# Time mixing of each 128 rows moved into a later attention loop, in a Perceiver block in float32

## The chip, the cores and the metric

The kernel runs on one core of a Trainium2 chip. The metric is the device time of one execution in microseconds (us); lower is better. Before the change the median of three runs is 2709.6 us (2709.19 to 2710.01).

The engines that matter are TensorE (PE, with its weight loads, PEld), VectorE (DVE), ScalarE (ACT), GpSimd (POOL) and SyncE (SP), which issues nearly all DMAs. Each engine works through its own queue in order. Work that passes between engines waits on semaphores, which the Tile framework places.

## The reference

One Perceiver block: cross-attention, RWKV time mixing, and a feed-forward network (FFN), each behind a layer norm without gain and each added back to x. x is (32, 64, 256), the context is (32, 1601, 192), everything is float32.

```python
x = x + xattn(layernorm(x), ctx)          # 16 heads of 64, 1601 keys of 192
x = x + rwkv(layernorm(x))
x = x + ffn(layernorm(x))                 # relu(x @ w1 + b1) @ w2 + b2, width 1024

# xattn: q = query @ w_q, kv = ctx @ w_kv, softmax(q k^T / 8) v, then @ w_out + b_out
# rwkv:  shifted = x one step later in time (zeros first)
k_in = x * mix_k + shifted * (1 - mix_k)  # v_in and r_in likewise
k, v = k_in @ Wk.T, v_in @ Wv.T
r = sigmoid(r_in @ Wr.T)
td = exp(-exp(time_decay))
for t in range(64):
    e, ek = exp(time_first + k[t]), exp(k[t])
    wkv[t] = (num + e * v[t]) / (den + e)
    num, den = td * num + ek * v[t], td * den + ek
out = (r * wkv) @ Wo.T + bo
```

## The kernel before

x lies in SBUF for the whole run as `x_sb`, 16 tiles of 128 rows. One tile holds two batches of 64 queries.

**Queries** (to about 143.8 us). Four groups of 512 rows are normed, transposed and projected, and each head's query is multiplied with that head's key weights (`wkT`), so that the scores can be made from the 192 columns of the context itself. The folded queries go to DRAM (`q_dram`). `rstd_of` (L97) makes the inverse root of a variance: DVE adds epsilon, ACT takes the root, DVE the reciprocal. The constants of the time mixing (`rw_T`, `td_rows`, `omm`, `cols`) are made here too.

**Attention** (143.8 to 2485.44 us). The loop runs over 64 units u. Unit u is half a batch: b = u // 2, and of its 16 heads eight, j = u % 2, so 512 columns. Four units make a tile of x. The body of the loop works on two units at once, in this order of program:

- `last.total()`: DVE sums the exponentials of the unit before (L419, L421).
- `scores(u)`: six groups of 256 keys. Each has eight matmuls into a PSUM tile of two banks (L350; two such tiles, `ps_s`), a copy to SBUF by ACT (L357) and a running maximum by DVE (L359, L361). A seventh, small group holds the last 65 keys (L369). After the second group (i == 1) a hook is called, which runs `vproj` of the unit before the last, if that unit ended a tile.
- Loads of the next batch's context blocks and queries by SP.
- `max_all`: GpSimd takes the maximum over partitions (L387).
- `last.av_lo`: 13 chunks of keys, exponentials of the unit before times the first 128 context columns, into one PSUM bank `o_lo` (L432).
- `exps`: DVE subtracts the maximum (L393), ACT takes exponentials (L396, L399).
- `ctx_prep` for every second unit: DVE transposes the next batch's context (L257, L258).
- `last.av_hi`: the last 64 context columns into `o_hi` (L444, L454).
- `last.out`: the copies of `o_lo` (ACT, L473) and `o_hi` (DVE, L471) to `oT`, the denominators `den` by two matmuls (L477), and their reciprocal `rden` (L484).
- `vproj`, for every fourth unit u and two units later in the loop: 32 matmuls with the value weights into `v_ps` (L497), division by the denominators (L505), eight with the output weights into `y_ps` (L508), and two adds that bring the result into `x_sb` (L515, L516).

`den`, `v_ps` and `y_ps` share one PSUM pool, `ps_m`, of two banks, through the helper `bank`. With `ps_s` (four banks) and `o_lo` and `o_hi` all eight banks are in use.

**The tail** (2485.44 us to the end). Four stages of 512 rows (four tiles): `rwkv(nb)` does the time mixing of a stage, `ffn(nb)` the feed-forward, and the mixing runs one stage ahead. Within `rwkv` the order is norm (L584), transposes (L590) into `xp`, three mixed inputs (ACT `tmp` L609, DVE `in_` L612), projections (L621), exponentials (L642, L643), a sigmoid (L649), scans by DVE (L654), a reciprocal (L661), the products (L662, L663), and the output projection `ry` (L668), added into `x_sb`. `ffn` norms and transposes, makes `h_ps` (L689), the relu (L696), `fy` (L701), and writes the sums out by SP.

Program order on each engine is the order in which the instructions are written out; the framework moves nothing.

Of the kernel before, what the change touches and what calls it, by code (L numbers as in the profile page):

```python
# [9 lines left out]
F32 = mybir.dt.float32  # L10
# [5 lines left out]
P = 128  # L16
# [4 lines left out]
def kernel(  # L21
# [33 lines left out]

    nc = tc.nc
# [27 lines left out]
    nc.gpsimd.memset(ones, 1.0)  # L84

# [11 lines left out]
    def rstd_of(dst, var):  # L97
        nc.vector.tensor_scalar(dst, var, EPS, None, ALU.add)
        nc.scalar.activation(dst, dst, AF.Sqrt)
        nc.vector.reciprocal(dst, dst)  # L100
# [12 lines left out]
    with tc.tile_pool(name="aw", bufs=1) as aw:  # L113
        wv_lo = aw.tile([P, INNER], F32, name="wv_lo")
        wv_hi = aw.tile([P, INNER], F32, name="wv_hi")
        wo_sb = aw.tile([P, INNER // P, D], F32, name="wo_sb")

        with ExitStack() as st_a:
            cpool = st_a.enter_context(tc.tile_pool(name="ctx", bufs=1))

            kp = st_a.enter_context(tc.tile_pool(name="keys", bufs=2))
# [210 lines left out]
            ap = st_a.enter_context(tc.tile_pool(name="attn", bufs=1))  # L332
            ps_s = st_a.enter_context(tc.tile_pool(name="ps_s", bufs=2, space=PSUM))
            ps_o = st_a.enter_context(tc.tile_pool(name="ps_o", bufs=1, space=PSUM))
            ps_m = st_a.enter_context(tc.tile_pool(name="ps_m", bufs=2, space=PSUM))
# [4 lines left out]
            def scores(u, cT, q, hook):  # L340
# [4 lines left out]
                for i in range(KC // 2):  # L345
# [16 lines left out]
                    if i == 1:  # L362
                        hook()
# [159 lines left out]
            oT = rden = None  # L523
            for u in range(2 * B):
                b, j = divmod(u, 2)

                def finish(done=late):
                    if done is not None:
                        done.vproj()
# [3 lines left out]
                s_sb, mx = scores(u, cT, q_tiles[b], finish)  # L533
# [7 lines left out]
                if j == 0 and b + 1 < B:  # L541
                    cT_next = ctx_prep(b + 1)
                elif j == 1:
                    cT = cT_next
                if last is not None:
                    last.av_hi()
                    last.out()
                if j == 0:
                    c_tiles[b] = ctx_load(b)
# [5 lines left out]
            late.vproj()  # L555
            last.total()
            last.av_lo(0, NCK)
            last.av_hi()
# [3 lines left out]
    NB = 4  # L562
    TB = NT * P // NB
    BB = TB // T
    TT = TB // P
    NF = FF // P
    wp = ctx.enter_context(tc.tile_pool(name="fw", bufs=1))
    rp = ctx.enter_context(tc.tile_pool(name="rw", bufs=1))
    fp = ctx.enter_context(tc.tile_pool(name="ff", bufs=2))
    pp_t = ctx.enter_context(tc.tile_pool(name="pp_t", bufs=2, space=PSUM))  # L570
    pp_m = ctx.enter_context(tc.tile_pool(name="pp_m", bufs=4, space=PSUM))
    pp_y = ctx.enter_context(tc.tile_pool(name="pp_y", bufs=2, space=PSUM))

    w1_sb = wp.tile([P, 2, FF], F32, name="w1_sb")
    w2_sb = wp.tile([P, NF, D], F32, name="w2_sb")
    nc.sync.dma_start(w1_sb, w1.rearrange("(c p) f -> p c f", p=P))
    nc.sync.dma_start(w2_sb, w2.rearrange("(c p) d -> p c d", p=P))

    def normed(nb, name, dst):
        tiles = [nb * TT + k for k in range(TT)]  # L580
        mv, rstd = stats_of(fp, tiles, f"{name}_{nb}")
        xn = fp.tile([P, TT, D], F32, tag="xn", name=f"xn_{name}_{nb}")
        for k, i in enumerate(tiles):
            nc.vector.tensor_scalar(  # L584
                xn[:, k, :], x_sb[:, i, :], mv[:, k, 0:1], rstd[:, k : k + 1], ALU.subtract, ALU.mult
            )
        for c in range(2):
            pt = pp_t.tile([P, TT, P], F32, tag="t", name=f"xT_{name}_{nb}_{c}")
            for k in range(TT):
                nc.tensor.transpose(pt[:, k, :], xn[:, k, c * P : (c + 1) * P], ident)  # L590
            dst(c, pt)

    def rwkv(nb):
        xp = rp.tile([P, 2, BB, T + 1], F32, tag="xp", name=f"xp_{nb}", bufs=2)
        nc.gpsimd.memset(xp[:, :, :, 0:1], 0.0)

        def put(c, pt):
            nc.scalar.copy(
                xp[:, c, :, 1 : T + 1], pt.rearrange("p k (b t) -> p (k b) t", t=T)
            )  # L600

        normed(nb, "ln2", put)

        mixed = []
        for n, nm in enumerate(("k", "v", "r")):
            tmp = rp.tile([P, 2, BB, T], F32, tag="tmp", name=f"tmp_{nm}_{nb}", bufs=2)
            mi = rp.tile([P, 2, BB, T], F32, tag=f"in_{nm}", name=f"in_{nm}_{nb}", bufs=2)
            for c in range(2):
                nc.scalar.activation(  # L609
                    tmp[:, c], xp[:, c, :, 0:T], AF.Copy, scale=omm[:, n, c : c + 1]  # L610
                )
                nc.vector.scalar_tensor_tensor(  # L612
                    mi[:, c], xp[:, c, :, 1 : T + 1], cols[:, 2 + n, c : c + 1], tmp[:, c],
                    ALU.mult, ALU.add,
                )
            mixed.append(mi.rearrange("p c b t -> p c (b t)"))

        def proj(src, w, c, nm):
            ps = pp_m.tile([P, TB], F32, tag="mm", name=f"{nm}_ps_{nb}_{c}")
            for hc in range(2):  # L620
                nc.tensor.matmul(  # L621
                    ps,
                    lhsT=rw_T[w][:, hc, c * P : (c + 1) * P],
                    rhs=src[:, hc, :],
                    start=(hc == 0),
                    stop=(hc == 1),
                )
            return ps

        rw = rp.tile([P, 2, TB], F32, tag="rwv", name=f"rwv_{nb}", bufs=2)  # L630
        num = rp.tile([P, 2, BB, T + 1], F32, tag="num", name=f"num_{nb}")
        den = rp.tile([P, 2, BB, T + 1], F32, tag="den", name=f"den_{nb}")
        nc.gpsimd.memset(num[:, :, :, 0:1], 0.0)
        nc.gpsimd.memset(den[:, :, :, 0:1], 0.0)
        ek = rp.tile([P, 2, TB], F32, tag="ek", name=f"ek_{nb}")
        e = rp.tile([P, 2, TB], F32, tag="e", name=f"e_{nb}")
        ekv = rp.tile([P, 2, TB], F32, tag="ekv", name=f"ekv_{nb}")
        ev = rp.tile([P, 2, TB], F32, tag="ev", name=f"ev_{nb}")
        r = rp.tile([P, 2, TB], F32, tag="r", name=f"r_{nb}")
        for c in range(2):  # L640
            pk = proj(mixed[0], "Wk", c, "k")
            nc.scalar.activation(ek[:, c], pk, AF.Exp)  # L642
            nc.scalar.activation(e[:, c], pk, AF.Exp, bias=cols[:, 1, c : c + 1])  # L643
            pv = proj(mixed[1], "Wv", c, "v")
            nc.vector.tensor_tensor(ekv[:, c], ek[:, c], pv, ALU.mult)
            nc.vector.tensor_tensor(ev[:, c], e[:, c], pv, ALU.mult)
        for c in range(2):
            pr = proj(mixed[2], "Wr", c, "r")
            nc.scalar.activation(r[:, c], pr, AF.Sigmoid)  # L649
        for c in range(2):  # L650
            for b in range(BB):
                ts = slice(b * T, (b + 1) * T)
                for acc, src in ((num, ekv), (den, ek)):
                    nc.vector.tensor_tensor_scan(  # L654
                        acc[:, c, b, 1 : T + 1], td_rows[:, c, :], src[:, c, ts], 0.0, ALU.mult, ALU.add
                    )
            ev3 = ev[:, c].rearrange("p (b t) -> p b t", t=T)
            e3 = e[:, c].rearrange("p (b t) -> p b t", t=T)
            nc.vector.tensor_tensor(ev3, ev3, num[:, c, :, 0:T], ALU.add)
            nc.vector.tensor_tensor(e3, e3, den[:, c, :, 0:T], ALU.add)  # L660
        nc.vector.reciprocal(e, e)  # L661
        nc.vector.tensor_tensor(ev, ev, e, ALU.mult)  # L662
        nc.vector.tensor_tensor(rw, r, ev, ALU.mult)  # L663
        for k in range(TT):
            i = nb * TT + k
            py = pp_y.tile([P, D], F32, tag="y", name=f"ry_{nb}_{k}")
            for c in range(2):
                nc.tensor.matmul(  # L668
                    py,
                    lhsT=rw[:, c, k * P : (k + 1) * P],  # L670
                    rhs=rw_T["Wo"][:, c, :],
                    start=(c == 0),
                    stop=(c == 1),
                )
            nc.vector.tensor_tensor(x_sb[:, i, :], x_sb[:, i, :], py, ALU.add)
            nc.vector.tensor_tensor(x_sb[:, i, :], x_sb[:, i, :], bias_rows[:, 1, :], ALU.add)
# [37 lines left out]
    for nb in range(NB):  # L714
        if nb + 1 < NB:
            rwkv(nb + 1)
# [50 lines left out]
```

## Time and profile before

| | before |
|---|---|
| median of 3 runs | 2709.6 us (2709.19 to 2710.01) |
| the profiled execution: its own time | 2708.48 us |
| its span, first to last instruction | 2706.6 us |
| mean granted TensorE clock | 0.992 |
| busy in the span: PE / DVE / ACT / POOL | 2634.8 / 1891.5 / 974.8 / 122.9 us |
| queries, 0 to 143.80: PE busy | 123.12 us |
| attention, 143.80 to 2485.44: PE busy | 2329.17 of 2341.64 us, clock 1.00 |
| tail, 2485.44 to 2706.60: PE busy | 182.55 of 221.16 us, clock 0.93 |

The profile is of one execution, so its rows add up to its own time and not to the median. A group of instructions is shown with its line, engine, operation, output and inputs, number, total busy time and mean length of one, and the idle time that came just ahead of its instructions on their engine, with what ended it ("<-"). In a view by stretch, each engine has its busy time and, in brackets, its number of instructions; PEclk is the share of full clock that TensorE was granted. PE counts matmuls and transposes; the weight loads beside them are PEld.

### The profile page before, as it was taken

The page shows a single profiled execution, that of the slowest core. Times are in us where ns is not written, and L with a number is a line of the kernel's source. Part 1 is how long each engine was busy: PE and PEld are TensorE (multiplying, and loading weights), DVE is VectorE, ACT ScalarE, POOL GpSimd, SP SyncE. Part 2 cuts the span into 40 slices and gives each one's busy share as a digit, 9 for nine tenths or more (in the row PEclk, how much of TensorE's full clock was granted, in tenths as well). Part 3 has the DMA queues.
Part 4 walks back from the last instruction along what each step waited for, and adds up shares of the span by engine and source line. Part 5 has one row for each costly group of instructions (what it writes and reads, how often), then busy time and mean ns, then how long its engine had stood idle before and what let it go on. Part 6 is the DMA issues. An engine that isn't in the chain of part 4 may idle for free.

```text
span 2706.6 us, 27923 instructions
## 1 busy us (share of the span) xinstructions
PE 2634.8 (97%) x11424; PEld 1209.8 (45%) x11424; DVE 1891.5 (70%) x1983; ACT 974.8 (36%) x958; POOL 122.9 (5%) x92
## 2 busy tenths in 40 slices
PE   7979999999999999999999999999999999999699
PEld 3334444444444444444444444444444444444366
DVE  4467677776767776767677776767776767776864
ACT  2233333333333333323333333333333333333242
POOL 1000000000000000000000000000000000000000
PEclk9989999999999999999999999999999999999899
DMA  8983233332333331333333333333332323100000
GB/s 207 267 154 59 39 61 61 61 58 46 61 61 61 61 61 43 61 57 55 48 61 61 50 55 60 61 61 61 57 58 49 61 48 55 38 19 31 0 16 16
DMA packets 435279, 169.27 MB, mean 63 GB/s; under 512 B 330192, under 2 KB 421360, under 8 KB 435152
## 3 DMA queue, kind: packets, MB, share of 16 engines
q1 hardware_dynamic: 434272, 166.05, 32.4%
q8 instruction: 89, 1.46, 0.2%
q10 hardware_dynamic: 544, 1.05, 0.1%
q0 software_dynamic: 336, 0.40, 0.1%
q14 instruction: 38, 0.31, 0.0%
HBM read 138.60 MB, written 27.26 MB: 61 GB/s over the span
## 4 chain that ended last, share of the span: by engine, by line
PE 93%; DVE 4%; ACT 1%; issue 1%; DMA 1%; SPq 0%; POOL 0%; DVEq 0%; POOLq 0%; ACTq 0%
PE s_ps L350 37%; PE o_lo L432 27%; PE o_hi L444 13%; PE s_ps_r L369 3%; PE y_ps L508 2%; PE v_ps L497 2%; PE fy L701 2%; PE q_ps L192 2%; PE h_ps L689 1%; PE o_hi L454 1%; PE den L477 1%; DVE e L661 1%; PE ql_ps L208 1%; DMA q_dram<-q_hi 1%; PE qh_ps L223 0%
## 5 line engine op out<-in xcount | busy, mean ns | idle before, releaser
L350 PE MATMUL s_ps<-q,cT 64*128 64x512 f32 x4608 | 1013.5, 594 | 12.9 <-ACT s_sb L357 12.1
L357 ACT COPY s_sb<-s_ps 128x1024 f32<-128x1024 f32 x384 | 388.5, 1012 | 981.2 <-PE s_ps L350 981.2
L432 PE MATMUL o_lo<-s_sb,c 128*128 128x512 f32 (+1 forms) x1664 | 731.4, 596 | 0.0
L350 PEld LDWEIGHTS s_ps<-q,cT 64*128 64x128 f32 x4608 | 440.5, 187 | 549.8 <-issue 535.8
L361 DVE TENSOR_TENSOR m<-m,s_sb 128x1024 f32<-128x1024 f32 x256 | 313.7, 1225 | 368.3 <-ACT s_sb L357 368.3
L396 ACT ACTIVATE s_sb<-s_sb 128x2048 f32<-128x2048 f32 x192 | 366.7, 1911 | 454.3 <-DVE s_sb L393 454.3
L393 DVE TENSOR_TENSOR s_sb<-s_sb,mb 128x2048 f32<-128x2048 f32 x192 | 428.5, 2287 | 101.3 <-POOL mb L387 101.3
L432 PEld LDWEIGHTS o_lo<-s_sb,c 128*128 128x128 f32 (+1 forms) x1664 | 311.0, 190 | 392.0 <-issue 392.0
L444 PE MATMUL o_hi<-s_sb,c 128*64 128x512 f32 x1536 | 343.7, 596 | 0.0
L421 DVE TENSOR_TENSOR t<-t,s_sb 128x1024 f32<-128x1024 f32 x256 | 312.2, 1219 | 14.7 <-DVE t L421 0.5
L387 POOL PARTITION_ALL_REDUCE mb<-mx x64 | 114.2, 1785 | 2313.3 <-DVE mx L380 2313.3
L444 PEld LDWEIGHTS o_hi<-s_sb,c 128*64 128x64 f32 x1536 | 104.6, 137 | 231.2 <-issue 207.0
L359 DVE TENSOR_TENSOR m<-s_sb 128x1024 f32<-128x1024 f32 x64 | 78.4, 1225 | 92.7 <-ACT s_sb L357 92.6
L484 DVE RECIPROCAL rden<-den 128x256 f32<-128x256 f32 x64 | 111.8, 1748 | 0.0
L369 PE MATMUL s_ps_r<-q,cT 64*65 64x256 f32 x768 | 93.6, 376 | 0.0
L257 DVE STREAM_TRANSPOSE cT<-cb 128x768 f32<-128x768 f32 x96 | 92.7, 968 | 0.0
L419 DVE TENSOR_TENSOR t<-s_sb 128x1024 f32<-128x1024 f32 x64 | 77.7, 1214 | 0.0
L369 PEld LDWEIGHTS s_ps_r<-q,cT 64*65 64x65 f32 x768 | 54.0, 134 | 52.8 <-issue 33.5
L192 PE MATMUL q_ps<-xnT,wq_sb 128*128 128x512 f32 x128 | 60.5, 615 | 0.0
L508 PE MATMUL y_ps<-wo_sb,outT 128*128 128x256 f32 x256 | 59.5, 386 | 0.0
L689 PE MATMUL h_ps<-xT,w_sb 128*128 128x512 f32 x128 | 56.1, 594 | 0.6 <-ACT xT L682 0.6
L701 PE MATMUL fy<-w_sb,hT 128*128 128x256 f32 x256 | 55.9, 379 | 0.0
(124 smaller groups left out, 1415.2 us busy)
## 6 DMA issues: line engine op xcount, KB each, us to landing
q<-q_dram SPq DMA_DIRECT2D x64, 768.0 KB, 6.7
c<-in_ctx_dram SPq DMA_DIRECT2D x32, 1152.0 KB, 6.3
cb<-in_ctx_dram SPq DMA_DIRECT2D x192, 104.0 KB, 4.3
cb<-in_ctx_dram SPq DMA_DIRECT2D x192, 96.0 KB, 3.3
q_dram<-q_lo SPq DMA_DIRECT2D x16, 1024.0 KB, 8.8
q_dram<-q_hi SPq DMA_DIRECT2D x32, 256.0 KB, 6.8
x_sb<-in_x_dram SPq DMA_DIRECT2D x4, 512.0 KB, 8.6
w_sb<-in_L_ffn_w_dram SPq DMA_DIRECT2D x2, 1024.0 KB, 4.9
```

Of the source, the lines that this page charges most:

```text
L192: nc.tensor.matmul(pq, lhsT=wq_sb[:, c, hp * P : (hp + 1) * P], rhs=xnT[:, c, :], start=(c == 0), stop=(c == 1),)
L350: nc.tensor.matmul(ps[:, k, :], lhsT=cT[rs, s, i * P : (i + 1) * P], rhs=q[rs, s, js : js + HALF], start=(s == 0), stop=(s == NS - 1),)
L357: nc.scalar.copy(s_sb[:, 2 * i : 2 * i + 2, :], ps)
L361: nc.vector.tensor_tensor(m2, m2, s_sb[:, 2 * i : 2 * i + 2, :], ALU.max)
L369: nc.tensor.matmul(ps[0:KR, k, 0:HH], lhsT=cT[rs, s, NB1 * BL : KT + 1], rhs=q[rs, s, js + k * HH : js + (k + 1) * HH], start=(s == 0), st ...
L387: nc.gpsimd.partition_all_reduce(mb, mx, P, bass_isa.ReduceOp.max)
L393: nc.vector.tensor_tensor(s4, s4, mb.unsqueeze(1).to_broadcast([P, 4, HALF]), ALU.subtract)
L396: nc.scalar.activation(s4, s4, AF.Exp)
L421: nc.vector.tensor_tensor(t2, t2, p[:, 2 * i : 2 * i + 2, :], ALU.add)
L432: nc.tensor.matmul(self.po, lhsT=self.ctx[0:n, self.at[c], 0:P], rhs=self.s_sb[0:n, c, :], start=(c == 0), stop=(c == NCK - 1),)
L444: nc.tensor.matmul(self.ph[o * C2 : (o + 1) * C2, :], lhsT=self.ctx[:, self.at[c], P:C], rhs=self.s_sb[:, c, :], start=(c < 2), stop=False ...
L508: nc.tensor.matmul(py, lhsT=outT[:, k, :], rhs=wo_sb[:, k, :], start=(k == 0), stop=(k == NP - 1),)
```

## The change

- **`rstd_of`**: after DVE's add, GpSimd raises the variance to the power -0.5 with a constant tile `root`. ACT's root and DVE's reciprocal are gone. This holds for all layer norms.
- **Time mixing by tile.** `rwkv` is replaced by a class `Mixing` for one tile of 128 rows (two batches). It has five steps: `norm`, `mix`, `project`, `scan`, `out`. For tiles 0 to 14 they are put into the attention loop. Tile i's attention is complete when `vproj` has run in unit 4i+5; `norm` is at the end of that unit, `mix` in unit 4i+6 after the third group of scores (i == 2 in `scores`), `project` in unit 4i+7 between `av_lo` and `av_hi`, `scan` in the same unit after `out`, and `out` in unit 4i+8 after the third group of scores. `out` of tile 14 is behind the loop, between the last `av_lo` and `av_hi`.
- **PSUM of the mixing.** `mix`, `project` and `out` take their PSUM tiles from `ps_m`, the two banks that `den`, `v_ps` and `y_ps` also use. The projections of a tile are one bank for Wk, one for Wv and one for Wr.
- **Sigmoid.** r * wkv with r = 1 / (1 + exp(-k_r)) becomes a longer denominator: (1 + exp(-r)) * (e + den), with one reciprocal.
- **FFN.** The tail holds four `ffn` stages. Tile 15's mixing and the norms of stages 1 to 3 are called between pairs of its h matmuls, through the list `between`. Its PSUM is one bank for transposes, three for `h_ps`, two for `fy`.
- **Pools.** The SBUF pool of the mixing (`rw`) is opened ahead of attention; the attention weights (`aw`) move into the attention's own pools and are freed with them; `ps_m` stays open to the end.

The core of the diff (the removed `rwkv`, and the parts of the FFN that only moved, are cut):

```diff
+    root = const.tile([P, 4], F32, name="root")
+    nc.gpsimd.memset(root, -0.5)
...
     def rstd_of(dst, var):
         nc.vector.tensor_scalar(dst, var, EPS, None, ALU.add)
-        nc.scalar.activation(dst, dst, AF.Sqrt)
-        nc.vector.reciprocal(dst, dst)
+        nc.gpsimd.tensor_tensor(dst, dst, root[:, 0 : dst.shape[1]], ALU.pow)
...
+            class Mixing:
+                def __init__(self, i):
+                    self.i = i
+
+                def norm(self):
+                    i = self.i
+                    mv, rstd = stats_of(rp, [i], f"ln2_{i}")
+                    self.xn = rp.tile([P, D], F32, tag="xn", name=f"xn_ln2_{i}")
+                    nc.vector.tensor_scalar(
+                        self.xn, x_sb[:, i, :], mv[:, 0, 0:1], rstd[:, 0:1], ALU.subtract, ALU.mult
+                    )
+
+                def mix(self):
+                    i = self.i
+                    pt = bank([P, 2, 2, T], f"xT_ln2_{i}")
+                    for c in range(2):
+                        nc.tensor.transpose(pt[:, c, :, :], self.xn[:, c * P : (c + 1) * P], ident)
+                    xp = rp.tile([P, 2, 2, T + 1], F32, tag="xp", name=f"xp_{i}")
+                    nc.gpsimd.memset(xp[:, :, :, 0:1], 0.0)
+                    nc.scalar.copy(xp[:, :, :, 1 : T + 1], pt)
+                    self.mixed = []
+                    for n, nm in enumerate(("k", "v", "r")):
+                        tmp = rp.tile([P, 2, 2, T], F32, tag="e", name=f"tmp_{nm}_{i}")
+                        mi = rp.tile([P, 2, 2, T], F32, tag=f"in_{nm}", name=f"in_{nm}_{i}")
+                        for c in range(2):
+                            nc.scalar.activation(
+                                tmp[:, c], xp[:, c, :, 0:T], AF.Copy, scale=omm[:, n, c : c + 1]
+                            )
+                            nc.vector.scalar_tensor_tensor(
+                                mi[:, c], xp[:, c, :, 1 : T + 1], cols[:, 2 + n, c : c + 1],
+                                tmp[:, c], ALU.mult, ALU.add,
+                            )
+                        self.mixed.append(mi.rearrange("p c b t -> p c (b t)"))
+
+                def project(self):
+                    i = self.i
+
+                    def proj(n, w):
+                        ps = bank([P, 2, 2, T], f"{w}_ps_{i}")
+                        for c in range(2):
+                            for hc in range(2):
+                                nc.tensor.matmul(
+                                    ps[:, c, :, :],
+                                    lhsT=rw_T[w][:, hc, c * P : (c + 1) * P],
+                                    rhs=self.mixed[n][:, hc, :],
+                                    start=(hc == 0),
+                                    stop=(hc == 1),
+                                )
+                        return ps
+
+                    shape = [P, 2, 2, T]
+                    pk = proj(0, "Wk")
+                    pv = proj(1, "Wv")
+                    self.ek = rp.tile(shape, F32, tag="in_k", name=f"ek_{i}")
+                    self.e = rp.tile(shape, F32, tag="e", name=f"e_{i}")
+                    nc.scalar.activation(self.ek, pk, AF.Exp)
+                    for c in range(2):
+                        nc.scalar.activation(
+                            self.e[:, c], pk[:, c], AF.Exp, bias=cols[:, 1, c : c + 1]
+                        )
+                    self.ekv = rp.tile(shape, F32, tag="in_v", name=f"ekv_{i}")
+                    self.ev = rp.tile(shape, F32, tag="ev", name=f"ev_{i}")
+                    nc.vector.tensor_tensor(self.ekv, self.ek, pv, ALU.mult)
+                    nc.vector.tensor_tensor(self.ev, self.e, pv, ALU.mult)
+                    pr = proj(2, "Wr")
+                    self.er = rp.tile(shape, F32, tag="in_r", name=f"er_{i}")
+                    nc.scalar.activation(self.er, pr, AF.Exp, scale=-1.0)
+
+                def scan(self):
+                    i = self.i
+                    num = rp.tile([P, 2, 2, T], F32, tag="num", name=f"num_{i}")
+                    den = rp.tile([P, 2, 2, T], F32, tag="den", name=f"den_{i}")
+                    for acc, src in ((num, self.ekv), (den, self.ek)):
+                        for c in range(2):
+                            for b in range(2):
+                                nc.vector.tensor_tensor_scan(
+                                    acc[:, c, b, :], td_rows[:, c, :], src[:, c, b, :],
+                                    0.0, ALU.mult, ALU.add,
+                                )
+                    for to, acc in ((self.ev, num), (self.e, den)):
+                        nc.vector.tensor_tensor(
+                            to[:, :, :, 1:T], to[:, :, :, 1:T], acc[:, :, :, 0 : T - 1], ALU.add
+                        )
+                    nc.vector.scalar_tensor_tensor(
+                        self.e, self.er, 1.0, self.e, ALU.add, ALU.mult
+                    )
+                    nc.vector.reciprocal(self.e, self.e)
+                    self.rw = rp.tile([P, 2, P], F32, tag="xn", name=f"rwv_{i}")
+                    nc.vector.tensor_tensor(
+                        self.rw, self.ev.rearrange("p c b t -> p c (b t)"),
+                        self.e.rearrange("p c b t -> p c (b t)"), ALU.mult,
+                    )
+
+                def out(self):
+                    i = self.i
+                    py = bank([P, D], f"ry_{i}")
+                    for c in range(2):
+                        nc.tensor.matmul(
+                            py, lhsT=self.rw[:, c, :], rhs=rw_T["Wo"][:, c, :],
+                            start=(c == 0), stop=(c == 1),
+                        )
+                    ...  # two adds into x_sb
...
-                    if i == 1:
+                    for hook in hooks.get(i, ()):
                         hook()
...
+                hooks = {}
+                if late is not None:
+                    hooks[1] = [late.vproj]
+                phase, i = (u - 5) % 4, (u - 5) // 4
+                mixer = mixing.get(i)
+                if phase == 1 and mixer:
+                    hooks[2] = [mixer.mix]
+                elif phase == 3 and mixer:
+                    hooks[2] = [mixer.out]
...
+                if phase == 2 and mixer:
+                    mixer.project()
                 if last is not None:
                     last.av_hi()
                     last.out()
+                if phase == 2 and mixer:
+                    mixer.scan()
+                elif phase == 0 and i >= 0:
+                    mixing[i] = Mixing(i)
+                    mixing[i].norm()
...
             last.av_lo(0, NCK)
+            mixing[NT - 2].out()
             last.av_hi()
...
+        def ffn(nb, xT, between):
...
+                nc.scalar.activation(hT[:, f, :], ps, AF.Relu, bias=b1_sb[:, f : f + 1])
+                if between and f % 2 == 1:
+                    between.pop(0)()
...
+        mixer = Mixing(NT - 1)
+        xTs = {0: normed(0)}
+        mixer.norm()
+        norms = {
+            nb: lambda nb=nb: xTs.update({nb: normed(nb)}) for nb in range(1, NB)
+        }
+        steps = (
+            [mixer.mix, norms[1], mixer.project, mixer.scan],
+            [mixer.out, norms[2]],
+            [norms[3]],
+            [],
+        )
+        for nb in range(NB):
+            ffn(nb, xTs[nb], list(steps[nb]))
```

## The prediction

> **What bounds the kernel now.** I read the head of the page first (who is busy), then the chain that ended last, then busy time by stretch, then TensorE's waits, and last one unit of attention in order of time.
>
> ```profile
> span 2706.6 us, 27923 instructions
> PE 2634.8 (97%) x11424; PEld 1209.8 (45%) x11424; DVE 1891.5 (70%) x1983; ACT 974.8 (36%) x958; POOL 122.9 (5%) x92
> ...
> PE 93%; DVE 4%; ACT 1%; issue 1%; DMA 1%; SPq 0%; POOL 0%; DVEq 0%; POOLq 0%; ACTq 0%
> ```
>
> TensorE carries 93% of the chain. The stretches say where it doesn't. The first three rows are attention units (58, 59 and 61; 61 also has the output projection of a tile), the last is all that follows attention, from the end of the last y_ps.
>
> ```profile
> core 0: us, PE busy (x) PEld busy (x) DVE busy (x) ACT busy (x) POOL busy (x), PEclk, DMA share, GB/s
> 2245.79:2280.26 34.47, 34.47 (x145) 14.79 (x143) 26.04 (x22) 13.38 (x12) 1.78 (x1) 1.00 0.38 37
> 2280.26:2314.73 34.47, 34.47 (x145) 14.80 (x143) 25.45 (x24) 13.38 (x12) 1.78 (x1) 1.00 0.37 83
> ...
> 2349.20:2391.24 42.04, 42.04 (x226) 21.21 (x224) 26.55 (x25) 13.38 (x12) 1.78 (x1) 1.00 0.11 30
> 2485.44:2706.60 221.16, 182.55 (x608) 112.20 (x608) 145.65 (x374) 75.86 (x116) 1.28 (x12) 0.93 0.06 19
> ```
>
> In attention TensorE has no gap at all (34.47 of 34.47), at full clock. Whatever is put there costs its TensorE time in full, and every wait of TensorE too. In the tail TensorE idles 38.6 us, and part of its work runs at a lower granted clock. Its waits there (total, number, longest):
>
> ```profile
> PE ry L668 <- DVE rwv L663: 15.4, 3, 12.3
> PE k_ps L621 <- DVE in_k L612: 12.2, 4, 5.8
> PE xT_ln L590 <- DVE xn_ln L584: 5.5, 1, 5.5
> ```
>
> All three belong to the time mixing. So the change trades this idle time for whatever waits it brings into a loop that has none. One unit (59, an odd one like those that get the projections), TensorE and ScalarE (start, length, instruction; in brackets the idle time ahead of it):
>
> ```profile
> 2297.20 11.43 PE L432 MATMUL o_lo<-s_sb,c 128*128 128x512 f32 x26
> 2308.56 5.37 PE L444 MATMUL o_hi<-s_sb,c 128*64 128x512 f32 x24
> 2311.07 0.61 ACT L399 ACTIVATE s_sb<-s_sb 65x512 f32<-65x512 f32 x1
> 2311.59 0.57 ACT L473 COPY oT<-o_lo 128x512 f32<-128x512 f32 x1
> 2313.76 0.60 PE L454 MATMUL o_hi<-s_sb,c 65*64 65x256 f32 x4
> 2317.62 1.01 ACT L357 COPY s_sb<-s_ps 128x1024 f32<-128x1024 f32 x1 [5.46 <-PE s_ps L350]
> ```
>
> The reader should see that when o_lo ends (2308.56) ScalarE still has its exponentials and the copy of o_lo to do, until 2312.16. Then it is idle 5.46 us.
>
> **What goes.** After the last y_ps: four rwkv stages, table loads and all waits above. What stays: four FFN blocks; the undisturbed one of the chain runs from 2674.98 (h_ps) to 2702.81 (end of fy), 27.83 us, so 4 x 27.83 = 111.3. The transposes of ln3, 32 at 0.11 us (8 in 0.86 in the tail), 3.5. The mixing of tile 15, among FFN's matmuls: 3.7 us of TensorE (below). At the start, transposes and their two copies (0.59 each) alternate on one PSUM buffer: 0.9 of idle; the order of the built kernel shows the first norms on DVE ahead of the last y_ps, and the load of w1 and w2 waiting only for the last scores, over 40 us ahead, so it is hidden (without that cover two loads of 1 MB at 4.9 us to landing, about 10). The end, last fy to end of span, 3.8 as now. Together 123.2, against 221.2: **98.0 us gained**, with 3 either way (tile 15's chain could stop an FFN block once or twice).
>
> **What comes into the loop**, 15 times (tiles 0 to 14), each spread over four units. The TensorE work is what it was: 2 transposes 0.22; 24 passes over 128 columns at 0.11, 2.6; 4 passes of out at 0.218 (16 of y_ps in 3.49), 0.87; sum 3.7. Before, the 96 passes of a stage at 0.43, 16 of ry and 8 transposes make 59 for 16 tiles, the same. The rest is seams and waits:
>
> - mix (third unit): transposes between two score groups. Scores are 64-row matmuls, transposes use the whole array; the seam from scores to v_ps costs 0.20 (24 passes last 5.35 instead of 24 x 0.2144), that from y_ps back 0.16. With 0.22 that is 0.58. ScalarE then does xp and three pairs of tmp, each pair waiting for DVE's in_ pair of the one before (one buffer, tag e), and behind them in its queue stand the copies that free the PSUM of scores. By 0.37 for xp, 0.33 for a tmp, 0.31 for an in_ (rows of 512 columns scaled, 0.2 fixed) and m2 of 1.23 ahead on DVE, copy 3 ends 4.2 us after copy 2 instead of 2.57; score group 5 needs it 4.0 us after, plus the 0.36 of seams: wait 0 (0 to 1).
> - project (fourth unit): Wk and Wv after o_lo, 0.86 each, one o_hi matmul alone, 0.86, then Wr, which takes the PSUM buffer of Wk (two in ps_m). That is free only when ScalarE has done e, and ek and e stand in its queue behind the exponentials and the copy of o_lo: ek from 2312.06, e in two halves, the last ending at 2312.96. TensorE is there at 2308.56 + 2.6 = 2311.1 and waits until 2313.0, 1.9 us. Behind this wait stand the rest of o_hi, den and the next scores. Then Wr 0.86 and its first weights 0.1, seam 0.19, and o_hi goes on at 5.7 us after o_lo, with 0.45 of it done: 5.25 us added (4.8 to 5.7).
> - out (first unit of the next four): 0.87 and two seams, 1.21. rwv is done some 3 us earlier on DVE.
> - norm (second unit): no TensorE work. DVE waits for GpSimd's pow, and behind it stand the maxima of scores. x_sb is ready at 2362.8 in unit 61's times, pow could start at 2363.4, the next maximum is due at 2365.78, and DVE idles 1.35 per score group after that: a pow of up to 1.9 us costs nothing, up to 7 can be caught up. No row shows pow; the nearest are a POOL memset of one column (0.10) and the 1.78 of L387. I take 0 (0 to 0.5).
>
> Sum 0.58 + 5.25 + 1.21 = 7.04 a tile, **105.6 us lost** in 15. DVE gains about 10 us in 145 of which it is idle 43.
>
> **GpSimd.** The order shows an unnamed instruction ahead of each pow and another ahead of the next reduction (L387): a change of code. The trace has two such places:
>
> ```profile
> 13.62 0.28 POOL masks.py:199 TENSOR_SCALAR_AFFINE_SELECT ident<-ident 128x128 f32<-128x128 f32 x1 [11.44 <-issue]
> ...
> 165.92 1.81 POOL L387 PARTITION_ALL_REDUCE mb<-mx  x1 [146.29 <-DVE mx L380]
> ```
>
> The first was waited for, 11.44 us at most; the second fell into idle time, and the first reduction then took 1.81 against 1.78. So a change takes its time where it stands in the queue, not at first use. The one ahead of pow has 30 us of idle POOL; the one after has from about 2364 to the last maximum at 2376.2, 12 us, and a late reduction first eats ScalarE's 5.46 idle and 1.56 of the second score buffer. Cost 0 until a change takes 19 us.
>
> The Trainium skill (GPSIMD Engine Reference, 2.1 Instruction dispatch) says otherwise: the first call of freshly loaded code pays about 6 us, with no instruction to see. By it pow and reduction would be 6 us late each, 6.3 together after DVE has caught up, still under 7.0, and the sum would not change.
>
> At the start the four square roots become pows; the first sits behind ident (13.9), so xn and the copies of wkT after it on DVE come 0.1 to 1 us later: 0.4.
>
> **Sum.** -98.0 + 105.6 + 0.4 = +8.0. The profiled execution took 2708.48 (span 2706.6), 1.1 under the median of 2709.6. Forecast 2717.5. Its own range, from the bounds above (15 times 0.5, and 3 of the tail), is 2706 to 2730. Measurement can tell about 5.4 us, 0.2%.
>
> **Rivals.** *The wait at Wr is not there* (other side: faster). If ScalarE freed Wk's buffer before TensorE came, project would cost its 2.6 and no more, a tile 4.4, 15 of them 66: 2678. Break-even is 6.5 a tile, so it decides from 0.5 us less wait than I have; half the wait gone gives about 2703. For it: my ScalarE times for short shapes are scaled. Against: the exponentials alone last to 2311.68 in the row. *Code changes paid at first use*: with R each, DVE is late by R - 5.7 and the reduction by R more, and TensorE feels what is over 7.0: it decides at R = 6.4, and at 11.4 costs 10.1 x 15 = 152, 2869. Against: the 1.81. *Everything cancels*: 6.5 a tile, 2705 to 2715.
>
> **Chances.** Forecast, more than 0.2% slower, 0.50; code changes 0.06; cancelling 0.20; faster 0.24. The range takes in the forecast, the cancelling and the half-gone wait, and above it 1 us more of waiting per tile: 2697 to 2742.
>
> **What would show it.** Right: TensorE's wait list has Wr <- ACT e, 15 times near 1.9; four units last 152 to 153 instead of 145.38; the tail after the last y_ps is 123. Wrong: no such wait (faster), units of the norm longer with DVE or ACT waiting on POOL (code changes), or a tail over 130.

## The result and the profile after

The changed kernel takes 2713.3 us (median of 22 runs, 2711.8 to 2717.0), the kernel before 2708.7 us in runs beside it (22, 2704.8 to 2711.8). The ratio is 1.0018, with a 95% interval of 1.0012 to 1.0023: a small loss, 4.6 us, where the forecast was +8. The profiled execution took 2715.08 us, with a span of 2713.3, so it lies 1.8 us above its median; the stretches below are from it.

One sentence above is wrong. I wrote that program order is the order in which the instructions are written out and that the framework moves nothing. The framework reorders: in the trace of the kernel before DVE's sums of `total` run between the context transposes of the unit before, and in that of the changed kernel one chunk of `o_hi` stands ahead of Wr, though `project` is written out ahead of `av_hi`. The prediction's steps used the order of the built kernel.

The head of the page and the chain of the changed kernel; TensorE is busy 24.9 us longer, and its share of the chain is 7 points lower:

```profile
PE 2659.7 (98%) x11712; PEld 1236.2 (46%) x11712; DVE 1906.7 (70%) x2123; ACT 975.1 (36%) x1051; POOL 141.4 (5%) x121
...
PE 86%; DVE 6%; ACT 2%; DMA 2%; issue 2%; POOL 1%; SPq 1%; DVEq 0%; POOLq 0%; ACTq 0%
```

The span cut at the y_ps matmuls tells where the time went:

| | first y_ps of tile 0 starts | from there to the last y_ps | after it, to the end |
|---|---|---|---|
| before | 322.9 | 2162.2 | 221.1 |
| after | 313.9 | 2274.0 | 125.0 |
| difference | -9.0 | +111.8 (7.45 a tile) | -96.1 |

The sum is +6.7, the difference of the two spans. Next come three of the four units of one tile, cut where `s_ps` starts (`mix`, `project`, `out`), and the tail. The columns are length, then busy time of PE, PEld, DVE, ACT and POOL, TensorE's clock, and DMA share and rate:

```profile
2334.67:2369.89 35.22, 35.22 (x146) 14.84 (x144) 27.90 (x28) 15.63 (x19) 1.89 (x2) 1.00 0.30 37
2369.89:2409.88 39.99, 38.41 (x169) 18.05 (x167) 31.13 (x38) 14.55 (x16) 1.78 (x1) 1.00 0.30 71
2409.88:2445.61 35.73, 35.73 (x147) 15.40 (x146) 25.79 (x25) 13.38 (x12) 1.78 (x1) 1.00 0.01 2
2588.30:2713.30 125.00, 118.66 (x447) 79.14 (x444) 32.08 (x99) 29.75 (x51) 3.69 (x4) 1.00 0.05 17
```

A unit without the mixing takes 34.47 (in the kernel before). So `mix` costs 0.75, `project` 5.52 and `out` 1.26 us, 7.5 in all, and of the three only `project` has TensorE idle (39.99 - 38.41 = 1.58). The tail runs at full clock. TensorE's waits in the whole span (total, number, longest) show the predicted one, 15 times 1.53 us:

```profile
PE Wr_ps L386 <- ACT e L402: 22.9, 15, 1.6
...
PE xT_ln L718 <- ACT xT L721: 2.5, 2, 1.9
```

That place in the order of time on TensorE, and then on ScalarE:

```profile
2398.10 1.05 PE L386 MATMUL Wk_ps<-in_k,Wk_T 128*128 128x128 f32 x8
2398.99 1.06 PE L386 MATMUL Wv_ps<-in_v,Wv_T 128*128 128x128 f32 x8
2399.98 1.07 PE L559 MATMUL o_hi<-s_sb,c 128*64 128x512 f32 x2
2402.63 1.16 PE L386 MATMUL Wr_ps<-in_r,Wr_T 128*128 128x128 f32 x8 [1.58 <-ACT e L402]
2403.72 4.93 PE L559 MATMUL o_hi<-s_sb,c 128*64 128x512 f32 x21
```

```profile
2400.71 0.61 ACT L514 ACTIVATE s_sb<-s_sb 65x512 f32<-65x512 f32 x1
2401.22 0.56 ACT L588 COPY oT<-o_lo 128x512 f32<-128x512 f32 x1
2401.69 0.38 ACT L400 ACTIVATE ek<-Wk_ps 128x256 f32<-128x256 f32 x1
2401.97 0.61 ACT L402 ACTIVATE e<-Wk_ps,cols 128x128 f32<-128x128 f32 x2
```

The reader should see that the end of `e` (2402.58) releases Wr (2402.63), and that `e` is late because ScalarE is at the attention's exponentials and the copy of `o_lo` until 2401.78. On GpSimd the power and the reduction that follows it:

```profile
2307.30 0.60 POOL L102 TENSOR_TENSOR rstd_ln<-rstd_ln,root 128x1 f32<-128x1 f32 x1 [27.56 <-DVE rstd_ln L101]
2320.63 1.80 POOL L502 PARTITION_ALL_REDUCE mb<-mx  x1 [12.73 <-DVE mx L495]
```

The power starts at once when DVE has the variance (2307.20), and the reduction 0.22 us after the maximum (2320.41), though GpSimd changes code ahead of both; a change falls into the 27.56 and 12.73 us of idle time there.

### The profile page after: what moved, and what is told of

Same layout as the page of the kernel before. It is cut to its first block, busy times and chain, and to the rows that moved or that the text cites. A ratio compares the mean times of both kernels' runs of the same rounds, so it can differ in the third digit from the quotient of the medians.

```text
span 2713.3 us, 28792 instructions
## 1 busy us (share of the span) xinstructions
PE 2659.7 (98%) x11712; PEld 1236.2 (46%) x11712; DVE 1906.7 (70%) x2123; ACT 975.1 (36%) x1051; POOL 141.4 (5%) x121
## 4 chain that ended last, share of the span: by engine, by line
PE 86%; DVE 6%; ACT 2%; DMA 2%; issue 2%; POOL 1%; SPq 1%; DVEq 0%; POOLq 0%; ACTq 0%
PE s_ps L465 37%; PE o_lo L547 21%; PE o_hi L559 12%; DVE s_sb L508 4%; PE s_ps_r L484 2%; PE v_ps L612 2%; PE fy L744 2%; PE y_ps L623 2%; PE h_ps L730 2%; PE q_ps L195 2%; PE o_hi L569 1%; PE den L592 1%; POOL mb L502 1%; DVE m L476 1%; PE Wr_ps L386 1%
## 5 line engine op out<-in xcount | busy, mean ns | idle before, releaser
L465 PE MATMUL s_ps<-q,cT 64*128 64x512 f32 x4608 | 1025.7, 597 | 9.8 <-ACT s_sb L472 9.0
L559 PE MATMUL o_hi<-s_sb,c 128*64 128x512 f32 x1536 | 359.7, 597 | 0.0
L599 DVE RECIPROCAL rden<-den 128x256 f32<-128x256 f32 x64 | 111.8, 1747 | 0.0
L752 DVE TENSOR_TENSOR o<-x_sb,fy 128x256 f32<-128x256 f32 x16 | 6.7, 421 | 77.8 <-PE fy L744 77.8
```

The costliest lines, as they stand in the source:

```text
L465: nc.tensor.matmul(ps[:, k, :], lhsT=cT[rs, s, i * P : (i + 1) * P], rhs=q[rs, s, js : js + HALF], start=(s == 0), stop=(s == NS - 1),)
L559: nc.tensor.matmul(self.ph[o * C2 : (o + 1) * C2, :], lhsT=self.ctx[:, self.at[c], P:C], rhs=self.s_sb[:, c, :], start=(c < 2), stop=False ...
```

## The experiments

The theory was that the loop pays 7 us a tile for seams and one wait, and the rivals were that the wait hides something else, or that GpSimd's code is what costs. Two questions came up with the result: the start, 9 us shorter, which the prediction did not have, and why removing the wait gains more than its length. The table has all runs; the ratio is to the kernel before on the same chip. The three columns behind the ratio are from one profiled execution of each. In the six kernels with the changed kernel's start (the first six rows) tile 0's y_ps starts between 311.9 and 315.0, so differences of up to 3 us there can be scatter.

| run | median us | ratio (95%) | tile 0's y_ps starts | a tile in the loop | after the last y_ps |
|---|---|---|---|---|---|
| after | 2713.3 | 1.0018 (1.0012 to 1.0023) | 313.9 | +7.45 | 125.0 |
| e1_wr_late | 2678.0 | 0.9889 (0.9874 to 0.9904) | 311.9 | +5.01 | 125.0 |
| e9_lone | 2690.2 | 0.9932 (0.9915 to 0.9948) | 313.1 | +5.85 | 125.0 |
| e4_seam | 2699.3 | 0.9960 (0.9947 to 0.9974) | 313.2 | +6.51 | 125.0 |
| e6_both | 2664.5 | 0.9832 (0.9819 to 0.9845) | 315.0 | +4.06 | 124.9 |
| e8_tail | 2661.2 | 0.9819 (0.9804 to 0.9834) | 313.0 | +4.06 | 123.6 |
| e2_sqrt | 2722.4 | 1.0049 (1.0036 to 1.0061) | 323.9 | +7.45 | 125.8 |
| e10_tail_root | 2717.2 | 1.0033 (1.0021 to 1.0044) | 315.2 | +7.45 | 125.8 |
| e3_before_one_pow | 2706.2 | 0.9991 (0.9982 to 1.0000) | 324.7 | 0 | 221.1 |
| e7_before_pow | 2706.3 | 0.9984 (0.9975 to 0.9993) | 310.6 | 0 | 231.3 |
| e5_pow_each | 2945.2 | one run | | | |

### The wait at Wr, and the lone chunk

Wr and `er` are taken out of `project` into a step of their own, `gate`, behind `o_hi` (in the code of this section "..." stands for lines left out):

```diff
...
                 if last is not None:
                     last.av_hi()
+                    if phase == 2 and mixer:
+                        mixer.gate()
                     last.out()
```

> The changed kernel with one edit: the Wr projection is issued behind the last o_hi matmul instead of ahead of o_hi. Theory (the wait at Wr is a wait for the bank of Wk, which ScalarE frees only after the exponentials of attention): the 15 waits of 1.53 us (22.9 in all) and the lone o_hi piece with its seams (about 0.2 each) go, 26 us in all: 2713.3 - 26 = about 2687, faster than the kernel before. Rival (the wait moves on): den then waits for the bank of Wv, which DVE must free, or ry waits for a later rwv, and the time stays at about 2713.

It takes 2678.0: the wait is gone and nothing comes in its place. But a tile is 2.44 us cheaper, and not only the 1.53 of the wait and a seam of about 0.2. TensorE from `o_hi` to `den`:

```profile
2365.59 5.37 PE L563 MATMUL o_hi<-s_sb,c 128*64 128x512 f32 x24
2370.79 0.60 PE L573 MATMUL o_hi<-s_sb,c 65*64 65x256 f32 x4
2371.32 1.16 PE L386 MATMUL Wr_ps<-in_r,Wr_T 128*128 128x128 f32 x8
2372.41 0.65 PE L596 MATMUL den<-sum,ones 128*64 128x256 f32 x4
```

Here `o_hi`'s 24 passes take 5.2 us without a break. To see whether the break itself costs, Wr went one chunk earlier, behind 11 of 12 (`between` is `gate`):

```diff
...
                     for c in range(KC):
+                        if between is not None and c == KC - 1:
+                            between()
```

> The run with Wr behind o_hi (2678), but with Wr one chunk earlier: behind 11 of the 12 o_hi chunks instead of behind all. No wait for the bank of Wk is left there, for the 11 chunks take over 4 us. Theory (o_hi's chunks write two halves of the partitions and run in pairs, 24 passes in 5.2 us, so a piece with an odd number of chunks runs one of them alone, 0.86 instead of 0.43 us, and what follows is shifted by half a pair; this is what the run with Wr behind o_hi gained beyond the wait of 1.53 us): 0.5 to 0.9 us a tile more than with Wr behind all, 8 to 14 us: 2686 to 2692. Rival (the gain beyond the wait came from elsewhere, DVE or ScalarE): the same as with Wr behind o_hi, 2678.

The time is 2690.2, with no wait at Wr at all, and a tile costs 0.84 us more:

```profile
2377.77 5.36 PE L565 MATMUL o_hi<-s_sb,c 128*64 128x512 f32 x22
2383.07 1.16 PE L386 MATMUL Wr_ps<-in_r,Wr_T 128*128 128x128 f32 x8
2384.16 0.64 PE L565 MATMUL o_hi<-s_sb,c 128*64 128x512 f32 x1
```

22 passes take 5.3 us, about as long as 24 did, since the last of the 11 chunks runs alone: in the trace its two weight loads start one by one, at 2381.69 and 2382.12, where those before them start in twos every 0.43 us. The seams are no rival for this, for Wr stands between two matmuls of 64 columns of weights in both runs. So the break costs 0.84 and the wait 1.53, together 2.37 of the 2.44.

### The seams of mix and out

```diff
-                if phase == 1 and mixer:
-                    hooks[2] = [mixer.mix]
-                elif phase == 3 and mixer:
-                    hooks[2] = [mixer.out]
...
+                if phase == 1 and mixer:
+                    mixer.mix()
+                elif phase == 3 and mixer:
+                    mixer.out()
                 mb = max_all(u, mx)
```

> The changed kernel with one edit: the transposes of mix and the ry matmuls of out are issued between the last score group and o_lo, no longer between the third and fourth score groups. Theory (most of mix's 0.76 us and a part of out's 1.27 are seams between 64-row and 128-row matmuls, and o_lo has that seam anyway): mix falls to 0.25, out to 0.9, so 0.9 us for each of 15 tiles, 13 us: about 2700. Rival (the seam is no cost; what counts is ScalarE's and DVE's work behind the transposes, which now stands ahead of the exponentials): no gain, or a loss where the exponentials come more than 7 us late: 2713 or more.

It takes 2699.3, and a tile is 0.94 us cheaper. The transposes now take their own 0.27 and no second seam:

```profile
2338.23 0.44 PE L361 MATMUL xT_ln<-ident,xn_ln 128*128 128x128 f32 x2
2338.50 11.33 PE L547 MATMUL o_lo<-s_sb,c 128*128 128x512 f32 x26
```

ScalarE's work behind them does no harm there: the wait list of TensorE has nothing new in it. Both edits together:

> The changed kernel with both edits of the two runs that gained: Wr behind o_hi, and mix and out between the last score group and o_lo. Theory (the two costs are separate): the gains add, -35 and -14 from 2713, so 2664. A tile then costs about 3.0 for project, 0.27 for mix and 1.0 for out, 4.3 in all, near its 3.7 us of matmul work. Rival (both edits remove the same slack on ScalarE or PSUM): less than 10 us below 2678.

The gains add: it takes 2664.5. A tile costs 4.06 us, of which 3.7 is matmul work. Then the tail, with two PSUM banks for transposes (`pp_t`) and two for h (`pp_m`):

```diff
-        pp_t = st_b.enter_context(tc.tile_pool(name="pp_t", bufs=1, space=PSUM))
-        pp_m = st_b.enter_context(tc.tile_pool(name="pp_m", bufs=3, space=PSUM))
+        pp_t = st_b.enter_context(tc.tile_pool(name="pp_t", bufs=2, space=PSUM))
+        pp_m = st_b.enter_context(tc.tile_pool(name="pp_m", bufs=2, space=PSUM))
```

> As the run with both edits, and in the tail two PSUM banks for the FFN's transposes and two for h, instead of one and three. Theory (the tail's 1.8 us above the forecast are TensorE's two waits for ScalarE to empty the one transpose bank, 2.5 us): those waits go and the time falls by 1 to 3 us. Rival (with two banks h waits for the relu of 0.69 us every 0.86 us, now and then behind other work): the same or up to 5 us more.

The two waits on the transpose bank, 2.6 us, are gone, and one of 0.7 for a relu has come; the tail is 1.3 us shorter. The other 2 us between the two profiled executions are in the start, where nothing was changed. The total, 2661.2, is the lowest of all, but its interval overlaps that of the run with both edits.

### The start, and GpSimd's code

The changed kernel with the root as before:

```diff
-        nc.gpsimd.tensor_tensor(dst, dst, root[:, 0 : dst.shape[1]], ALU.pow)
+        nc.scalar.activation(dst, dst, AF.Sqrt)
+        nc.vector.reciprocal(dst, dst)
```

> The changed kernel with the inverse root as before (ScalarE's root, DVE's reciprocal), no GpSimd power anywhere. Theory (the start is 7.5 us shorter because an execution that ends with the code of the power on GpSimd leaves it loaded for the next one, whose first affine_select needs the same code): the last GpSimd code is again the reduction's, the first transpose starts at about 14 us instead of 9.1, the first scores 7 us later, and with a few us for table loads in the tail the time is 2720 to 2728. In the loop the root costs nothing. Rival (the start is short for another reason, such as the order of instructions): the first transpose stays at 9 us, 2713 to 2720.

It takes 2722.4. The gain at the start is gone (323.9), and affine_select is again preceded by 11.38 us of idle time. In the loop the root costs nothing (7.45). So the power is worth 9.1 us by the medians, nearly all of it at the start (the tail has 0.8). Which part of it does that? First, code left loaded: in the kernel before, the last norm alone takes the power:

```diff
...
-        rstd_of(rstd, mv[:, :, 1])
+        rstd_of(rstd, mv[:, :, 1], power=name == "ln3_3")
```

> The kernel before with one edit: the last of its norms (ln3 of the last stage) takes the power on GpSimd instead of ScalarE's root. Nothing at the start is changed but a small memset. Theory (code left loaded by the execution before): the first transpose starts at about 9 us instead of 13.95, the first scores 4 to 7 us earlier, 2702 to 2705 against 2708.7. Rival (the start is shorter because its own four norms take the power, or for the order of instructions): no change, 2709, or some us longer for the code change ahead of the last norm.

GpSimd at the start of that kernel:

```profile
2.55 0.30 POOL masks.py:199 TENSOR_SCALAR_AFFINE_SELECT ident<-ident 128x128 f32<-128x128 f32 x1 [0.36 <-issue]
```

The idle time ahead of affine_select is 0.36 us, where the kernel before had 11.44. Nothing at the start was changed but a memset, so the code that an execution leaves behind is there for the next. But it gains little: DVE then waited for x until 15.22, with the copies of wkT behind that, and TensorE waited 3.8 us for them. The first scores were 2.1 us earlier, tile 0's y_ps not earlier at all in this execution, the slowest of the eleven. The median is 2.7 us lower, between what the theory and the rival gave, with an interval of the ratio that reaches 1. The opposite case, power at the start and root in the tail, so that the reduction's code is left:

```diff
...
-        rstd_of(rstd, mv[:, :, 1])
+        rstd_of(rstd, mv[:, :, 1], power=name[:3] != "ln3" and name != f"ln2_{NT - 1}")
```

> The changed kernel with ScalarE's root and DVE's reciprocal in the norms of the tail only (ln3, and ln2 of tile 15); the start and the loop keep the power. The last GpSimd code of an execution is then the reduction's, so the start pays the change of code again, but with the power in its norms. Theory (the start's 9.0 us have two parts: 4.9 from the code left loaded, seen in the first transpose, and the rest from the norms by power, without a table load in the first unit's exponentials): the first transpose at 13.9 us, y_ps of tile 0 at 317 to 320 us, against 313.9 and, before, 322.9. Rival (without the loaded code nothing is left of it): y_ps of tile 0 at 322 to 325. The time is 2713 plus the loss at the start plus 0 to 6 us for table loads in the tail, 2717 to 2728.

The time, 2717.2, lies at the lower end of its range, but neither value for y_ps fits: affine_select has 10.84 us of idle time ahead again, yet tile 0's y_ps starts at 315.2, only 1.3 later than in the changed kernel and 8.7 earlier than with roots (e2_sqrt). So in these executions nearly all of the gain comes from the four norms at the start by power. The larger part of it shows in unit 1, here in the kernel before, TensorE and ScalarE:

```profile
178.40 13.32 PE L350 MATMUL s_ps<-q,cT 64*128 64x512 f32 x48 [10.95 <-ACT s_sb L357]
170.13 1.28 ACT L396 ACT_TABLE_LOAD   x1 [7.29 <-DVE s_sb L393]
```

and in the changed kernel:

```profile
169.35 13.42 PE L465 MATMUL s_ps<-q,cT 64*128 64x512 f32 x48 [6.05 <-ACT s_sb L472]
168.31 0.99 ACT L472 COPY s_sb<-s_ps 128x1024 f32<-128x1024 f32 x1
```

With roots, ScalarE loads a table (1.28) ahead of unit 0's exponentials and does all of them in a row ahead of unit 1's first score copy, and TensorE waits 10.95 us for that copy. With the power the copy stands behind the first exponential, without a load, and the wait is 6.05. That is 4.9 of it; why the copy is placed earlier no run shows.

The code left loaded does bring the first scores forward, from 140.46 (e10_tail_root) to 136.25, 4.2 us. Most of that is lost again in unit 0: in the changed kernel ScalarE's first score copies wait for a load of context (11.76 us of idle time) until 143.57, where e10_tail_root has them at 146.22. TensorE waits 2.96 us for them instead of 1.40, and in the next 4.4 us it was granted 0.63 of its clock, where e10_tail_root has 1.00. By the medians the loaded code is worth more than these 1.3 us: 2.7 in e3_before_one_pow, and some 3 in e10_tail_root (3.9 above the changed kernel, with 0.8 of it in the tail). So the split of the 9 us between the two is open within about 2 us.

Last, the power in all norms of the kernel before, nothing else:

```diff
...
-        nc.scalar.activation(dst, dst, AF.Sqrt)
-        nc.vector.reciprocal(dst, dst)
+        nc.gpsimd.tensor_tensor(dst, dst, root[:, 0 : dst.shape[1]], ALU.pow)
```

> The kernel before with all its norms by GpSimd's power, nothing else: one part of the change alone. Theory (the start's 7.5 us come from this part: code left loaded, and the order of DVE's copies that follows from it): first scores at about 136 us instead of 143.8, 8 us less at the start; in the tail the table loads for the root go (8 norms), which frees 0 to 10 us: 2692 to 2702. Rival (the start's gain needs the moved mixing): first scores at 142 to 144 us, 2700 to 2709.

The start gains 12.3 us (310.6), but the total, forecast at 2692 to 2702, only 3.7 (2706.3 against 2710.0 beside it). The tail takes 10.2 back:

```profile
2473.50 0.13 POOL L596 MEMSET xp<- 128x16 f32 x1
2485.36 2.18 POOL L101 TENSOR_TENSOR rstd_ln<-rstd_ln,root 128x4 f32<-128x4 f32 x2 [11.72 <-issue]
```

The change of code to the power is queued behind memsets that wait for the last y_ps (2473.2), so it stands on the path: 11.72 us of idle time, and TensorE's wait for the first norm grows from 5.5 to 13.8. In the changed kernel the same change has 27 to 42 us of idle GpSimd (ahead of the norm shown above, and ahead of the first norm of the tail). The change back, put on the path in every unit:

```diff
...
+                nc.gpsimd.tensor_tensor(one, mx[:, 0:1], mx[:, 0:1], ALU.subtract)
+                nc.gpsimd.tensor_tensor(one, ones[:, 0:1], one, ALU.pow)
+                nc.gpsimd.tensor_tensor(mx[:, 0:1], mx[:, 0:1], one, ALU.mult)
                 mb = ap.tile([P, HALF], F32, tag="mb", name=f"mb_{u}")
```

> The changed kernel with three small GpSimd operations put ahead of each of the 64 reductions, on one column of its input: a subtraction, a power of one (to the zero), and a product, so that the result is the same. GpSimd's code then has to change twice a unit, the second time between the maximum and the reduction that waits for it. Theory (a change takes its time where it stands in GpSimd's queue, up to 11.4 us, the idle time ahead of the first affine_select of the kernel before): between the product and the reduction lie 6 to 11 us; what goes over 7 us is felt by TensorE: 0 to 6 us for each of 64 units, 2715 to 3110. Rival (a change costs next to nothing, and the start was late for something else): the reduction follows within 1 us, 2713 to 2720.

It takes 2945.2 in one run, 3.6 us a unit more:

```profile
1516.97 0.19 POOL L502 TENSOR_TENSOR one<-mx 128x1 f32<-128x1 f32 x1 [12.61 <-DVE mx L496]
1517.24 0.55 POOL L503 TENSOR_TENSOR one<-ones,one 128x1 f32<-128x1 f32 x1
1517.88 0.19 POOL L504 TENSOR_TENSOR mx<-mx,one 128x1 f32<-128x1 f32 x1
1523.88 1.80 POOL L506 PARTITION_ALL_REDUCE mb<-mx  x1 [5.81 <-issue]
```

Between the product and the reduction lie 5.81 us here, 6.00 and 6.30 in the next units. With the three operations the reduction is some 7 us late. The unit with `out` does not feel it (35.74, from 1617.15 to 1652.89, against 35.73), as forecast for less than 7 us. The units with `mix`, `project` and `vproj` do: their waits grow (39.7 us in all instead of 22.9 at Wr, 61.4 for outT, 71.4 for score copies), and TensorE's mean granted clock falls to 0.965. The Trainium skill (GPSIMD Engine Reference, 2.1 Instruction dispatch) has about 6 us for the first call of freshly loaded code. The size agrees for the reduction; ahead of the power the idle time was 11.72. It is paid where the change stands in the queue: in the changed kernel the reduction after a change started 0.22 us after its input.

## Why the prediction was right

The direction, and the mechanism of the loop, were right. Three sizes were off, and that the total comes so near is luck: the loop lost 6.2 us more and the tail gained 1.9 less than forecast, and the start, whose mechanism was missed, gave 9.4 back.

- **Loop, forecast 7.04 a tile, measured 7.45.** The wait of Wr on `e` is there 15 times, 1.53 us instead of 1.9. `out` is 1.26 (1.21), `mix` 0.75 (0.58): the seam back from transposes was a bit dearer. `project` is 5.52 (5.25) in spite of the shorter wait. `o_hi` goes on 5.62 us after Wk starts, near the 5.7 of the forecast, whose own terms add up to only 5.6 (4.44 until 2313.0, then 0.86, 0.1 and 0.19): the shorter wait is made up by pieces that each took somewhat more than 0.86. The mis-sized term is the one `o_hi` chunk ahead of Wr. I took 0.86 for it and counted 0.45 as done. Nothing was: from there to the next scores 6.16 us pass (2403.72 to 2409.88), where before the whole of `o_hi` and `den` took 6.17 (2308.56 to 2314.73). The run with 11 chunks shows the same, a loss of 0.84.
- **Tail, forecast 98.0 gained, measured 96.1.** The FFN blocks and tile 15 are as worked out; the norm transposes wait for the one PSUM bank 2.5 us instead of 0.9, and the tail is 125.0 and not 123.2.
- **Start, forecast 0.4 lost, measured 9.0 gained.** This is the step that failed: the term of 0.4 had the wrong size and the wrong sign. I looked at where the power stands on GpSimd and not at what goes from ScalarE: the roots, their table loads, and with them the order of the first exponentials. I also took the 11.44 us ahead of affine_select for a fixed cost, where the last code of the previous execution decides it (0.36 against 11.44).
- **GpSimd.** Right: changes of code cost nothing in this loop, since they are paid at their place in the queue and have 12 us or more there in the units shown. The rival of a late payment falls with the reduction that starts on time.
- **The rival without the wait at Wr** was priced at 2678, and the run without it took 2678.0. That agreement is partly luck too: a tile costs 5.01 there and not 4.4, 9 us in all, which the start gives back.
- **The range.** The bounds named for the forecast's own range, 7.5 and 3 us, make 2707 to 2728, not 2706 to 2730.

The forecast of +8 came out of +105.6, -98.0 and +0.4; the measured +6.7 of the profiled spans (+4.6 by the medians) out of +111.8, -96.1 and -9.0.

## What to carry to other kernels

Moving a stage with idle time into a loop whose engine has none gains only if the stage brings little more than its bare work: here 4.06 us a tile was affordable (3.7 is its matmul work), 7.45 was not, and of the 3.75 above the bare work 3.4 were taken out by placing the pieces at seams that were there anyway and one projection where its PSUM bank was free and the pairs of passes stayed whole. Count passes that run in pairs as pairs: a break behind an odd number of chunks cost 0.84 us here, as much as another pair (0.86). When an operation changes engines, look also at what the engine that loses it does at its next table load.

## What the runs showed of the hardware

- GpSimd's code outlives an execution: the idle time ahead of the first affine_select was 10.84 to 11.44 us where an execution ends with the reduction's code (before, e2_sqrt, e10_tail_root), and 0.36 where it ends with the power's (all others).
- A change of GpSimd's code on the path took 11.72 us towards the power and 5.81 to 6.30 towards the reduction.
- `o_hi`'s chunks, which write two halves of the partitions in turn, run two at a time: 24 passes of 512 columns in 5.2 us, where the 26 of `o_lo`, which use all partitions, take 11.3; with one chunk split off, 0.84 us more.
